# The product of wq and wo as 128 more columns of the gates' product

## The chip, the cores and the metric

The kernel runs on one core of a Trainium2 chip. The metric is the time of one execution on the device in microseconds (us); lower is better. Engines are named by their short names: PE is TensorE (matrix products), PEld its loading of weights, DVE is VectorE, ACT is ScalarE, POOL is GpSimd and SP is SyncE, which here only starts transfers.

## The reference, cut to what matters

Two layers, each a sum of an attention-like part and a feed-forward part over 8 x 256 tokens of 128 features. The first layer is a state-space block and a ternary feed-forward net. The second layer, in which the change lies, is:

```python
xn = _layernorm(x)
x  = x + attn(xn) + moe(xn)

# attn: per head (16 heads of 64), chunks of 64 tokens, W and b are a state that each chunk updates
xq, xk, xv = xn @ wq, xn @ wk, xn @ wv
Z1 = xk_c @ W + b;  lr = sigmoid(xk_c @ theta + theta_bias);  eta = token_eta * lr / 64
W, b = W - (eta * xk_c).T @ grad_x, b - sum(eta * grad_x)
Zq = xq_c @ W + b
out_c = xq_c + gamma * normalise(Zq) + beta
attn = concat(out) @ wo

# moe: 8 experts, the best 2 of each token by sigmoid(xn @ gate_w.T + gate_b), and a shared expert
```

Two consequences matter here. The term xq_c in out_c goes through wo unchanged, so its share of the result is xn @ (wq @ wo), a product with one matrix of 128 x 128. And the logits of the experts (8 columns) and of the rates lr (16 columns, from wk and theta) are also products of xn with a small matrix.

## The kernel before

The tokens are held as four chunks n (NCH) of four pairs of sequences bp (NBP): a tile is 128 rows, two sequences by 64 tokens. x1[n] is the residual stream of a chunk, 128 x 4 x 128 in SBUF; xnT[n] is its normalised and transposed form. All numbers are fp32.

The first layer runs first, with the order of all engines written out by hand (manual_schedule over all engines). Each chunk's feed-forward net is a list of steps (ffn_steps): first (two products and a silu), hidden (products and a gelu), mix and join, which end in residual, which adds the result to x1[n], and norm, which makes xnT[n] and lets POOL add the constant kc to x1[n]. Then come gates, scores and rates, the routing of the chunk's tokens: gates multiplies xnT[n] by gw, whose 24 columns are 8 for the experts and 16 for the rates; scores adds the bias and takes the sigmoid; rates makes eta and calls choose(0), the first choice of an expert; choose(1) makes the second choice and a product pn (all_ones and earlier times sel) that counts tokens; find_slots makes the slots from it. A function given to later() is put on a list that the next flush() runs, so gates, scores, rates and choose(1) come one flush apart, with steps of other work between them.

The chunks' steps are fillers in a main loop of turns. There are 16 units (chunk n, pair bp), and turn u works on three of them at once: z (unit u) makes states and gradients, g (unit u - 1) updates W and applies the queries, o (unit u - 2) writes out. For o the turn calls outputs_T (transposes the outputs, PE's poT and ACT's copy oT), then open_mix, mix_heads and residual:

```python
self.po = bank("po1")[:, :D]                       # open_mix: the opener, xn @ (wq wo)
nc.tensor.matmul(self.po, lhsT=xnT[self.n][:, self.bp, :], rhs=wqo, start=True, stop=False)
...                                                # mix_heads: eight products, oT by wo, into po
nc.vector.tensor_tensor(x, x, self.po, ALU.add)    # residual: x1[n][:, bp] += po
```

In the main loop the order of DVE and SP is the program's; that of PE, ACT and POOL is found by a scheduler that works with estimated times. The last turns are by hand again, for PE and ACT too. In turns 4, 5 and 14 to 16 the shared expert's pieces (shared_steps: a first part, pm and hid, and a second part, py) come in as fillers, in turn 5 also the routing of all tokens, and from turn 6 on the routed experts.

PSUM has two pools: bank() hands out one of four banks of 2 KB, two_banks() one of two pairs. A bank that is wanted waits until the last reader of an earlier tile in it is done. SBUF tiles named resident stay for the whole kernel: wqo, the product of wq and wo, is made once after the first layer and copied by ACT from PSUM.

Of the kernel before, what the change touches and what calls it, by code (L numbers as in the profile page):

```python
# [14 lines left out]
ALU = mybir.AluOpType  # L15
AX = mybir.AxisListType

P = 128
B, S, D = 8, 256, 128
# [4 lines left out]
H, HD, K = 16, 64, 64  # L24
HH = H // 2
NCH = S // K
NBP = B // 2
HC = H * HD
E = 8
# [31 lines left out]

C_EW2, C_EB1, C_EB2 = FF, 2 * FF, 2 * FF + 4
NEW = C_EB2 + D
I32 = mybir.dt.int32


# [12 lines left out]
def tile_two_layers(ctx: ExitStack, tc: tile.TileContext, t: dict, out: bass.AP):  # L79
    nc = tc.nc  # L80
# [10 lines left out]
    def bank(name):  # L91
        return ps1.tile([P, 512], F32, tag="bank", name=name)
# [4 lines left out]
    def resident(name, shape):  # L97
        return const.tile(shape, F32, tag=name, name=name)

    def resident_i(name, shape):  # L100
        return const.tile(shape, I32, tag=name, name=name)

    def load(name, shape, pool=const):
        sb = pool.tile(shape, F32, tag=name, name=name)
        nc.sync.dma_start(out=sb, in_=t[name])
        return sb
# [44 lines left out]
    x1 = [resident(f"x1_{n}", [P, NBP, D]) for n in range(NCH)]  # L151
    xnT = [resident(f"xnT_{n}", [P, NBP, P]) for n in range(NCH)]
# [27 lines left out]
    def later(f):  # L180
        pending.append(f)

    def flush():
        now, pending[:] = pending[:], []
        for f in now:
            f()
# [42 lines left out]
    gb = resident("gb", [P, E + H])  # L229

    def empty_rows(pool):
# [9 lines left out]
    nc.gpsimd.iota(  # L241
        second.bitcast(I32), [[P, NT]], base=B * S, channel_multiplier=1
    )
    nc.gpsimd.tensor_copy(second, second.bitcast(I32))
    wgt = resident("wgt", [P, NT, 2])
    eta = resident("eta", [P, NCH, NBP, H])
    te = resident("te", [P, 1])
    kc = resident("kc", [P, D])
    gw = resident("gw", [P, E + H])

    ready = []
    placed = []
# [13 lines left out]
    def ffn_steps(n):  # L266

        s = {}
# [58 lines left out]
        def norm():  # L327
            s["row"] = const.tile([P, NBP, ROW], F32, tag="xn1", name="xn1")
            s["xn"] = s["row"][:, :, 0:D]
            ln_apply_T(x1[n], s["stats"], s["xn"], xnT[n])  # L330
            nc.gpsimd.tensor_copy(s["row"][:, :, D], second[:, mine])
            nc.gpsimd.tensor_tensor(x1[n], x1[n], kc[:, None, :].to_broadcast([P, NBP, D]), ALU.add)
            later(gates)

        def gates():
            s["pg"] = bank("pg")[:, : NBP * (E + H)].rearrange("p (b c) -> p b c", b=NBP)
            for bp in range(NBP):
                nc.tensor.matmul(s["pg"][:, bp, :], lhsT=xnT[n][:, bp, :], rhs=gw, start=True, stop=True)
            later(scores)

        def scores():
            sg = small.tile([P, NBP, E + H], F32, tag="sg", name="sg")
            nc.vector.tensor_tensor(
                sg, s["pg"], gb[:, None, :].to_broadcast([P, NBP, E + H]), ALU.add
            )
            nc.scalar.activation(sg, sg, AF.Sigmoid)
            later(lambda: rates(sg))

        def rates(sg):
            nc.vector.tensor_scalar(eta[:, n], sg[:, :, E : E + H], te, None, ALU.mult)  # L350
            s["s"] = sg[:, :, 0:E]
            work = const.tile([P, 7, NBP * E], F32, tag="rt", name="rt")
            s["w"] = [work[:, i, :] for i in range(7)]
            choose(0)
            later(lambda: choose(1))

        def t_e(ap):
            return ap.rearrange("p (t e) -> p t e", e=E)
# [6 lines left out]
        def choose(k):  # L365

            shape = [P, NBP, E]
            left = t_e(s["w"][2]) if k else s["s"]
            m = wgt[:, mine, k]
            nc.vector.tensor_reduce(m, left, AX.X, ALU.max)  # L370
            eq = t_e(s["w"][k])
            nc.vector.tensor_tensor(eq, left, m.unsqueeze(2).to_broadcast(shape), ALU.is_equal)
            nc.vector.tensor_tensor(eq, eq, rank[:, None, :].to_broadcast(shape), ALU.mult)
            mr = small.tile([P, NBP], F32, tag="tk_mr", name="tk_mr") if k else s["row"][:, :, D + 1]
            nc.vector.tensor_reduce(mr, eq, AX.X, ALU.max)
            nc.vector.tensor_tensor(eq, eq, mr.unsqueeze(2).to_broadcast(shape), ALU.is_equal)
            if k == 0:
                nc.vector.scalar_tensor_tensor(t_e(s["w"][2]), eq, -4.0, s["s"], ALU.mult, ALU.add)
            else:
                sel = s["w"][3]  # L380
                nc.vector.tensor_tensor(sel, s["w"][0], s["w"][1], ALU.add)
                s["pn"] = bank("pn")[:, : 2 * NBP * E].rearrange("p (a c) -> p a c", a=2)
                nc.tensor.matmul(s["pn"][:, 0, :], lhsT=all_ones, rhs=sel, start=True, stop=True)
                nc.tensor.matmul(s["pn"][:, 1, :], lhsT=earlier, rhs=sel, start=True, stop=True)
                later(find_slots)
# [36 lines left out]
    with (  # L422
# [29 lines left out]
        wo = load("wo", [P, HH, D])  # L452
        headT = load("headT", [P, 2, HH], l0)
        wqT = load("wqT", [P, HH, D], l0)
        wq = load("wq", [P, HC])
        shared_w = resident("shared_w", [P, NEW])
        nc.sync.dma_start(out=shared_w, in_=t["moe_w"][E * P : NE * P, :])
        empty = empty_rows(l0)
        hp = [l0b.tile([P, B, S + 3], F32, tag="hp", name="hp") for half in range(2)]
# [54 lines left out]
        def convolve(half):  # L514
# [11 lines left out]
            return ins  # L526

        steps = ffn_steps(0)
        stats = {}
        layernorm0(0)  # L530
# [41 lines left out]
        for two in range(NBP // 2):  # L572

            pxp = bank("pxp").rearrange("p (b s) -> p b s", b=2)
            for half in range(2):
                for i in range(2):
                    b = 2 * (2 * two + i)
                    nc.tensor.matmul(
                        pxp[i * 64 : i * 64 + 64], lhsT=xp_w[:, half, :], rhs=hs[half][:, b : b + 2, :],
                        start=(half == 0), stop=(half == 1),  # L580
# [70 lines left out]
        for step in steps[12:14]:  # L651
            step()
        ffn1 = ffn_steps(1)

        pf = bank("pf")
        for hp_ in range(HH):
            nc.tensor.matmul(
                pf[:, 0:D], lhsT=wqT[:, hp_, :], rhs=wo[:, hp_, :], start=(hp_ == 0), stop=(hp_ == HH - 1)
            )
        wqo = resident("wqo", [P, D])  # L660
        nc.scalar.copy(wqo, pf[:, 0:D])

        pf2 = bank("pf2")[:, 0:D]
        for hp_ in range(HH):
            nc.tensor.matmul(
                pf2, lhsT=bpad[:, hp_, :], rhs=wo[:, hp_, :], start=(hp_ == 0), stop=(hp_ == HH - 1)
            )
        steps[14]()
        nc.vector.scalar_tensor_tensor(kc, shared_w[:, C_EB2:NEW], 0.1, pf2, ALU.mult, ALU.add)
        flush()  # L670
# [24 lines left out]
    def routing_steps():  # L695
        r = {}

        def work(name):

            return side["moe"].tile([P, NEW], F32, tag="ew", name=name, bufs=4)  # L700

        def constants():
            r["empty"] = empty_rows(side["moe"])
            w = r["w"] = work("rt_w")
            ints = w[:, 0:NJ].bitcast(I32)
            nc.gpsimd.iota(ints, [[1, NJ]], base=0, channel_multiplier=0)
# [110 lines left out]
    def expert_weights(j):  # L817
        if j < NJ:
            w = side["moe"].tile([P, NEW], F32, tag="ew", name=f"ew_{j}", bufs=4)
            r = nc.sync.value_load(wrow[0:1, j : j + 1], min_val=0, max_val=E * P)  # L820
# [11 lines left out]
    def routed_tokens_T(g):  # L832
        if g < NG:
            pt = bank("pxg")[:, : GJ * P].rearrange("p (j q) -> p j q", j=GJ)
            src = xg.pop(g)
            for j in range(GJ):
                nc.tensor.transpose(pt[:, j, :], src[:, j, 0:D], ident)
            ats[g] = side["moe"].tile([P, GJ], I32, tag="ats", name="ats", bufs=3)

# [42 lines left out]
    def routed_sums():  # L882
        for j, py in unsummed:
            g, i = divmod(j, GJ)
            if i == 0:
                ysum[g] = side["moe"].tile([P, GJ, D], F32, tag="ys", name="ys", bufs=3)
            nc.vector.tensor_tensor(ysum[g][:, i, :], py, ew.pop(j)[:, C_EB2:NEW], ALU.add)
            ready.append(lambda g=g, i=i: scatter_results(g, i))
        unsummed.clear()

    def scatter_results(g, i):
        assert g in known
        scattered.append(g * GJ + i)
        ins = transfer(
            out=y_dram, out_offset=bass.IndirectOffsetOnAxis(ap=ats[g][:, i : i + 1], axis=0),
            in_=ysum[g][:, i, :], in_offset=None, bounds_check=2 * B * S - 1, oob_is_err=False,
        )

        tc.declare_no_dep(ins, group="results", reason="distinct rows")
        tc.add_to_no_dep_group("results", ins)  # L900
# [23 lines left out]
    def result_steps(n, k):  # L924
# [3 lines left out]
        def fetch():  # L928
# [3 lines left out]
            elif n < NCH - 1:  # L932
                y = side["moe"].tile([P, NEW], F32, tag="ew", name="yc", bufs=4)[:, 0 : NBP * D]
            else:
# [38 lines left out]
    def pairs_of(heads):  # L973
        return slice(heads.start // 2, heads.stop // 2)
# [89 lines left out]
    class Unit:  # L1064
# [191 lines left out]

        def open_mix(self):
            self.po = bank("po1")[:, :D]
            nc.tensor.matmul(
                self.po, lhsT=xnT[self.n][:, self.bp, :], rhs=wqo, start=True, stop=False  # L1260
            )

        def mix_heads(self, k=ALL):
            part = pairs_of(k)
            for hp in range(part.start, part.stop):
                nc.tensor.matmul(  # L1266
                    self.po, lhsT=self.oT[:, hp, :], rhs=wo[:, hp, :], start=False,
                    stop=(hp == HH - 1),
                )

        def residual(self):
# [5 lines left out]
    fill = {u: [] for u in range(units + 2)}  # L1277
    gets = dict(RESULTS)
    steps = ffn1[EARLY:] + ffn_steps(2) + ffn_steps(3)
    for turn_u, k in FFN:  # L1280
        fill[turn_u] += [steps.pop(0) for _ in range(k)]
# [311 lines left out]
```

## Time and profile before

| what | us |
|---|---|
| median of 3 runs | 574.95 |
| lowest and highest | 573.02 and 576.1 |
| the profiled execution | 576.93 |
| its span, first to last instruction | 575.2 |
| PE busy in it | 534.9 |
| DVE busy in it | 405.0 |
| POOL busy in it | 296.3 |
| ACT busy in it | 259.0 |

The profile is that of one execution. A line of its timeline gives the start in us from the beginning of the span, the duration, the engine, the line of the kernel, the operation, what it writes and reads (output<-inputs), the shape, how many such instructions were merged (x16), and in brackets how long the engine had been idle before it and what ended that. A product in fp32 appears as two passes, so x2 is one product. Matrix passes overlap, and their ends are modelled, so their cost is read from the distance of their starts. A line of a table of stretches gives the stretch and its length, then for each of PE, PEld, DVE, ACT and POOL the busy time and the number of instructions, then the clock that PE was granted as a share of full speed, the share of the DMA engines' time, and GB/s.

### The profile page before, as it was taken

How to read it: one execution, taken by the hardware profiler on the slowest of the kernel's cores; microseconds unless marked ns; L12 is line 12 of the kernel's file. 1: busy time of each engine (PE TensorE's matmuls, PEld its weight loads, DVE VectorE, ACT ScalarE, POOL GpSimd, SP SyncE). 2: the span in 40 equal slices, each digit the busy share in tenths (PEclk: the TensorE clock that was granted, in tenths of full speed). 3: DMA queues.
4: the chain of work that ended last, by engine and by line, in shares of the span. 5: the costliest groups of instructions: out<-in, count | busy, mean ns of one | idle time of the engine just before them, and what ended most of it. 6: DMA issues, size and time to landing. Idle time of an engine off the chain costs nothing. (4 is left out here: it accounts for less than half of the span.)

```text
span 575.2 us, 14196 instructions
## 1 busy us (share of the span) xinstructions
PE 534.9 (93%) x5891; PEld 370.0 (64%) x5891; DVE 405.0 (70%) x649; ACT 259.0 (45%) x472; POOL 296.3 (52%) x258
## 2 busy tenths in 40 slices
PE   6999999999999999999978999999999999989695
PEld 3444655465556446476766787877787777878584
DVE  5597543647911675566969788869788777768995
ACT  5556444316420722314415363553546354453685
POOL 6216205750760176252774567465866646484861
PEclk9999999999999999898979999999999999999989
DMA  7901100000000000000152544352443434300322
GB/s 281 388 38 41 47 1 15 24 1 2 15 23 1 1 14 21 6 1 1 43 180 71 160 124 150 118 178 89 155 146 118 149 112 134 97 16 3 100 51 74
DMA packets 25200, 45.89 MB, mean 80 GB/s; under 512 B 3875, under 2 KB 16297, under 8 KB 24624
## 3 DMA queue, kind: packets, MB, share of 16 engines
q1 hardware_dynamic: 22864, 40.75, 21.9%
q0 software_dynamic: 2272, 4.24, 2.2%
q8 instruction: 46, 0.75, 0.5%
q14 instruction: 18, 0.15, 0.1%
HBM read 38.30 MB, written 7.13 MB: 79 GB/s over the span
## 5 line engine op out<-in xcount | busy, mean ns | idle before, releaser
L293 PE MATMUL pm<-g,h 128*128 128x512 f32 x256 | 115.3, 602 | 0.0
L175 POOL TENSOR_TENSOR rstd<-rs_v,neg_half 128x16 f32<-128x16 f32 x31 | 93.1, 3004 | 2.6
L293 PEld LDWEIGHTS pm<-g,h 128*128 128x128 f32 x256 | 48.7, 192 | 60.9 <-issue 58.1
L1118 POOL TENSOR_TENSOR gx<-xh,gam 128x1024 f32<-128x1024 f32 (+1 forms) x17 | 37.8, 2226 | 71.0 <-DVE er L1117 53.0
L866 ACT ACTIVATE rhid<-phd,ew 128x128 f32<-128x128 f32 x156 | 44.6, 373 | 41.3 <-issue 21.2
L174 POOL TENSOR_SCALAR rs_v<-var 128x16 f32<-128x16 f32 x31 | 7.3, 235 | 96.6 <-DVE var L1054 95.3
L297 ACT ACTIVATE g<-pm,cols 128x512 f32<-128x512 f32 x32 | 22.0, 687 | 77.1 <-PE pm L293 77.1
L163 POOL DMA_INDIRECT y_dram<-ys,ats x39 | 43.4, 1113 | 8.9 <-issue 8.8
L1054 DVE TENSOR_REDUCE var<-sq 128x16 f32<-128x1024 f32 (+1 forms) x33 | 38.9, 1181 | 9.4 <-ACT sq L1048 9.4
L861 PE MATMUL phd<-xgT,ew 128*128 128x128 f32 x312 | 43.4, 279 | 1.6 <-DMA ew<-in_moe_w 1.3
L861 PEld LDWEIGHTS phd<-xgT,ew 128*128 128x128 f32 x312 | 39.3, 191 | 8.0 <-issue 6.0
L1048 ACT ACTIVATE sq<-o 128x1024 f32<-128x1024 f32 (+1 forms) x17 | 17.1, 1009 | 55.1 <-DVE o L1037 55.1
L876 PE MATMUL pyr<-ew,rhid 128*128 128x128 f32 x312 | 41.4, 276 | 0.0
L163 POOL DMA_INDIRECT xg_dram<-xn,slot x32 | 35.9, 1121 | 8.6 <-issue 7.7
L1119 POOL TENSOR_TENSOR gx<-gx,u 128x1024 f32<-128x1024 f32 (+1 forms) x17 | 38.7, 2275 | 1.3
L876 PEld LDWEIGHTS pyr<-ew,rhid 128*128 128x128 f32 x312 | 38.0, 192 | 0.7 <-issue 0.5
L1094 DVE TENSOR_TENSOR u<-rows_b,pv 128x1024 f32<-128x1024 f32 x16 | 19.5, 1218 | 22.7 <-PE pv L982 22.7
L1266 PE MATMUL po<-wo,oT 128*128 128x128 f32 x256 | 33.1, 285 | 0.7 <-ACT oT L999 0.7
L1266 PEld LDWEIGHTS po<-wo,oT 128*128 128x128 f32 x256 | 32.0, 202 | 1.1 <-ACT oT L999 0.9
L982 PE MATMUL pk<-wk,xnT 128*128 128x512 f32 x64 | 31.4, 610 | 0.6 <-DVE xh L1037 0.4
L982 PE MATMUL pv<-wv,xnT 128*128 128x512 f32 x64 | 31.4, 613 | 0.0
L1011 PE MATMUL pq<-xnT,wq 128*128 128x256 f32 x128 | 30.8, 383 | 0.7 <-DVE B L1213 0.7
(233 smaller groups left out, 1067.7 us busy)
## 6 DMA issues: line engine op xcount, KB each, us to landing
ew<-in_moe_w SPq DMA_DIRECT2D x39, 578.0 KB
xg<-xg_dram SPq DMA_DIRECT2D x39, 65.0 KB
h<-in_h SPq DMA_DIRECT2D x2, 1024.0 KB
yc<-y_dram SPq DMA_DIRECT2D x6, 256.0 KB
rows_g<-in_rows_g SPq DMA_DIRECT2D x1, 1024.0 KB
rows_b<-in_rows_b SPq DMA_DIRECT2D x1, 1024.0 KB
w<-in_w SPq DMA_DIRECT2D x3, 256.0 KB
x<-in_x SPq DMA_DIRECT2D x3, 256.0 KB
```

Source lines behind the costliest of these rows:

```text
L163: ins = nc.gpsimd.indirect_dma_start(**what).ins
L175: turn[:] = [nc.gpsimd.tensor_tensor(dst, v[:, :width], neg_half[:, :width], ALU.pow).ins]
L293: nc.tensor.matmul(pm, lhsT=w[:, k, m * P : (m + 1) * P], rhs=s[src][:, k, :], start=(k == 0), stop=(k == 3),)
L861: nc.tensor.matmul(ph[:, ms], lhsT=w[:, ms], rhs=xgT[j // GJ][:, j % GJ, :], start=True, stop=True)
L866: nc.scalar.activation(hid[:, m, :], ph[:, ms], AF.Gelu, bias=w[:, C_EB1 + m : C_EB1 + m + 1])
L876: nc.tensor.matmul(py, lhsT=hid[:, m, :], rhs=w[:, C_EW2 + m * D : C_EW2 + (m + 1) * D], start=(m == 0), stop=(m == 3),)
L982: nc.tensor.matmul(pp[:, j, :], lhsT=xT, rhs=w[:, j * 512 : (j + 1) * 512], start=True, stop=True)
L1011: nc.tensor.matmul(pq[:, i, :], lhsT=wq[:, (h0 + i) * P : (h0 + i + 1) * P], rhs=xnT[n][:, 2 * half : 2 * half + 2, :], start=True, stop=True,
L1054: nc.vector.tensor_reduce(v[:, heads], sq[:, heads], AX.X, ALU.add)
L1118: nc.gpsimd.tensor_tensor(g, xh, gam2[:, k], ALU.mult)
L1119: turn[:] = [nc.gpsimd.tensor_tensor(g, g, self.t[:, k], ALU.add).ins]
L1266: nc.tensor.matmul(self.po, lhsT=self.oT[:, hp, :], rhs=wo[:, hp, :], start=False, stop=(hp == HH - 1),)
```

## The change

gw grows from 24 to 152 columns (NGW): its last 128 are the product of wq and wo, so wqo as a tile of its own goes. For chunks 0 to 2 gates multiplies by all 152 columns. Four pairs of 152 columns do not fit one bank of 512, so they go to two banks, two pairs in each; the bias is added in two halves. The product's last 128 columns are added to x1[n] by DVE in add_queries, two adds of 128 x 256, issued after choose(0) and ahead of choose(1). For these chunks open_mix only takes the bank, and the first product of mix_heads starts the sum. Chunk 3 keeps the narrow gates in one bank and its opener, which reads the 128 columns from gw.

```diff
+NGW = E + H + D
-    gw = resident("gw", [P, E + H])
+    gw = resident("gw", [P, NGW])
...
         def gates():
-            s["pg"] = bank("pg")[:, : NBP * (E + H)].rearrange("p (b c) -> p b c", b=NBP)
-            for bp in range(NBP):
-                nc.tensor.matmul(s["pg"][:, bp, :], lhsT=xnT[n][:, bp, :], rhs=gw, start=True, stop=True)
+            width, per = (E + H, NBP) if n == NCH - 1 else (NGW, 2)
+            s["pg"] = []
+            for b0 in range(0, NBP, per):
+                pg = bank("pg")[:, : per * width].rearrange("p (b c) -> p b c", b=per)
+                for i in range(per):
+                    nc.tensor.matmul(
+                        pg[:, i, :], lhsT=xnT[n][:, b0 + i, :], rhs=gw[:, 0:width], start=True, stop=True
+                    )
+                s["pg"].append((slice(b0, b0 + per), pg))
             later(scores)
         def scores():
             sg = small.tile([P, NBP, E + H], F32, tag="sg", name="sg")
-            nc.vector.tensor_tensor(
-                sg, s["pg"], gb[:, None, :].to_broadcast([P, NBP, E + H]), ALU.add
-            )
+            for pairs, pg in s["pg"]:
+                nc.vector.tensor_tensor(
+                    sg[:, pairs], pg[:, :, 0 : E + H],
+                    gb[:, None, :].to_broadcast([P, pg.shape[1], E + H]), ALU.add,
+                )
             nc.scalar.activation(sg, sg, AF.Sigmoid)
             later(lambda: rates(sg))
+        def add_queries():
+            for pairs, pg in s["pg"]:
+                x = x1[n][:, pairs, :]
+                nc.vector.tensor_tensor(x, x, pg[:, :, E + H : NGW], ALU.add)
         def rates(sg):
...
             choose(0)
             later(lambda: choose(1))
+            if n < NCH - 1:
+                add_queries()
...
-        wqo = resident("wqo", [P, D])
-        nc.scalar.copy(wqo, pf[:, 0:D])
+        nc.scalar.copy(gw[:, E + H : NGW], pf[:, 0:D])
...
         def open_mix(self):
             self.po = bank("po1")[:, :D]
-            nc.tensor.matmul(
-                self.po, lhsT=xnT[self.n][:, self.bp, :], rhs=wqo, start=True, stop=False
-            )
+            if self.n == NCH - 1:
+                nc.tensor.matmul(
+                    self.po, lhsT=xnT[self.n][:, self.bp, :], rhs=gw[:, E + H : NGW], start=True,
+                    stop=False,
+                )
...
-                    self.po, lhsT=self.oT[:, hp, :], rhs=wo[:, hp, :], start=False,
-                    stop=(hp == HH - 1),
+                    self.po, lhsT=self.oT[:, hp, :], rhs=wo[:, hp, :],
+                    start=(hp == 0 and self.n < NCH - 1), stop=(hp == HH - 1),
```

## The prediction

> **What bounds the kernel now.** I read the page first, then the waits of TensorE (PE), then the timeline around the lines that the change touches, then the order of instructions of the changed kernel as built, which shows what stands where on each engine and holds no times.
>
> ```profile
> PE 534.9 (93%) x5891; PEld 370.0 (64%) x5891; DVE 405.0 (70%) x649; ACT 259.0 (45%) x472; POOL 296.3 (52%) x258
> ...
> PEclk9999999999999999898979999999999999999989
> ```
>
> The span is 575.2 us, and PE is the bound: 93% busy; the clock line shows full speed nearly throughout. Its idle gaps over 0.08 us sum to some 30 us, and from 72 to 530 us hardly one is over 1.3 us, with one exception below. So PE time taken out there should come off the end, and DVE time (70%) should cost only where PE waits for it.
>
> What the change takes out and what it widens:
>
> ```profile
> 168.39 0.38 PE L1259 MATMUL po<-wqo,xnT 128*128 128x128 f32 x2
> 168.61 1.95 PE L1266 MATMUL po<-wo,oT 128*128 128x128 f32 x16
> ...
> 71.39 0.97 PE L338 MATMUL pg<-gw,xnT 128*128 128x24 f32 x8
> 71.39 0.86 PEld L338 LDWEIGHTS pg<-gw,xnT 128*128 128x128 f32 x7 [0.24 <-issue]
> ```
>
> A product in fp32 is two passes. The opener at 168.39 holds PE until the next product starts at 168.61: 0.22 us for two passes of 128 columns, 0.11 each. The durations in the second column include the drain of a pass and must not be summed. A pass of only 24 columns is no cheaper: seven weight loads in 0.86 us, six pitches in 0.67, again 0.11 us. So the weight load sets the pace of both.
>
> The exception, in turn 5 of the main loop (the turn in which the tokens are routed):
>
> ```profile
> 284.97 1.22 DVE L1247 TENSOR_TENSOR o<-o,rstd 128x1024 f32<-128x1024 f32 x1
> ...
> 286.33 0.72 PE L995 MATMUL poT<-ident,o 64*128 64x64 f32 x16
> ...
> 290.65 0.84 ACT L790 ACTIVATE hid<-pm,shared_w 128x256 f32<-128x256 f32 x2 [6.75 <-remote]
> 291.38 1.01 ACT L999 COPY oT<-poT 128x1024 f32<-128x1024 f32 x1
> 291.54 2.08 PE L784 MATMUL pm<-xnT,shared_w 128*128 128x256 f32 x4 [4.49 <-ACT hid L790]
> ```
>
> ScalarE (ACT) stands still for 6.75 us although its input has been ready since about 286.2; PE then stands for 4.49 us. The table of stretches shows the second price, the granted clock (the column before the last two):
>
> ```profile
> 289.00:292.40 3.40, 0.86 (x2) 0.77 (x3) 3.30 (x4) 1.74 (x3) 3.24 (x3) 0.50 0.29 83
> 292.40:295.80 3.40, 3.40 (x15) 3.13 (x15) 2.15 (x4) 0.84 (x2) 2.04 (x1) 0.50 0.76 243
> 295.80:299.00 3.20, 3.20 (x74) 3.08 (x76) 0.29 (x1) 0.00 (x0) 3.07 (x2) 1.00 0.94 336
> ```
>
> From 291.5 to 295.8 PE works at half speed: about 2.1 us lost.
>
> **The change part by part.** (1) Openers removed: 12 of 16 (chunks 0 to 2), 12 x 0.22 = -2.64 us. They lie in turns 2 to 13, where PE is the bound. (2) Gates widened: 12 products, 24 passes, from 24 to 152 columns. Passes of 512 columns follow each other at 0.43 us (16 of L293 in 7.03 us), so 152 columns are 0.127 us by proportion; with a little for issue I take 0.131, +0.02 each: +0.48 us. Ends: +0.016 (pure proportion) and +0.035. Here a rule speaks against the change. The Trainium skill, "TensorE: Matmul & The Clock Gate", section "Back-to-back issue gap", gives the isolated gap as columns over the clock plus a small constant, so work grows with columns. Scaled from our 0.43 us, 24 columns would have cost 0.02 us, and the widening 24 x 0.107 = 2.57 us: the whole saving gone. The row says 0.11 for the narrow pass, because every pass here loads new weights; I take the row. By the rule my sum would be 2.1 us later.
>
> (3) On DVE, per chunk: the add of the bias in two halves of 128x48 instead of one of 128x96 (0.258 us; a 128x32 takes 0.19), +0.15; and two adds of 128x256 from PSUM. The row L806 has this shape, two streams and a PSUM source: 0.416 us each. Together +0.98 us, three times 2.9 us, all before 200 us. They stand between choose(0) and choose(1). They also wait for GpSimd's add of kc to the same x1: it ended at 70.8, 131.3 and 192.0, five us before it is needed, so that wait is free. SyncE's and GpSimd's orders are unchanged; no DMA is added.
>
> (4) Buffers: the gates now take two of four PSUM banks and hold them until DVE has added the queries, not until the bias is added. Chunk 0: the next hidden product takes a bank that ACT must free (its silu ends at 74.04, later by the wider gates) and began at 74.00: I allow +0.25. Chunk 1: the scheduler has moved 29 of 32 products of z ahead of the pair that needs the bank. The adds end near 136.7 and 137.2, PE arrives at 136.9, and DVE's sel, 139.84 before, comes at about 140.4 for a PE that asks at 140.7: 0. Chunk 2 has no such cover:
>
> ```profile
> 197.86 0.74 DVE L283 SCALAR_TENSOR_TENSOR g<-p,cols,gs 128x512 f32<-128x512 f32 x1
> ...
> 199.63 0.19 DVE L381 TENSOR_TENSOR rt<-rt 128x32 f32<-128x32 f32 x1
> ...
> 199.88 0.41 PE L383 MATMUL pn<-rt,all_ones 128*128 128x32 f32 x2 [0.37 <-DVE rt L381]
> ```
>
> PE already waits here for DVE's sel, so everything added ahead of it on DVE shows: 0.85 for the adds and 0.16 for the shifted gates. sel moves from 199.82 to about 201.0. Behind pn wait the hidden products of chunk 3. Beyond the width, counted in (2), +1.0 us (0.4 to 1.8).
>
> (5) Turn 5 is reordered by the scheduler, because the opener no longer opens the bank early. In before the last shared pieces stood between the first shared product and poT: opener, second part, first part. Now poT and the output product follow directly, and one first part and one second part of the shared expert go behind z. PE is through at 282.9 and poT needs o, ready at 286.2: a hole of 3.4 us. poT is then done at 287, and the output product needs ACT's oT. If ACT stands until 290.6 as before, oT is there at 291.7, PE idles another 4.7 us, and the half clock runs to 295.8 again. Then output product, second part, first part (4.5 us of work, 2.05 us for the clock), so pw starts at 298.2 as before, but with 0.9 + 1.8 us of shared work still to do. That work fills the 1.6 us of gaps that before has between 302 and 307.5. Net +1.5 us (0 to +5).
>
> Is ACT's stand really going to come again? In the window 289 to 291 of the DMA view there is one packet on an instruction queue, and ACT goes on shortly after:
>
> ```profile
> q14 instruction: 1, 0.01, 2.4%
> ```
>
> So it looks like a late load of code, behind the writes of empty rows and scattered rows of those microseconds. The Trainium skill, "Runtime: NRT & Kernel Launch", section "Instruction fetch mechanics", calls the crossing of a code block mostly hidden. By that rule the stand would be an accident and gone in the new run. The trace shows 6.75 us; ACT's instruction count is the same and so is the traffic, so I let it return.
>
> (6) Elsewhere two expert products instead of one stand between output product and pw in three turns: 0.22 us, just the place that the opener had. Nothing.
>
> Sum: -2.64 + 0.48 + 0.25 + 1.0 + 1.5 = +0.6 us on a profiled execution of 576.93 us (span 575.2 and 1.7 around it). On the median of 574.95 us: 575.5.
>
> **The rivals.** A (likeliest): the saving on PE is spent in chunk 2 and turn 5: 575.5, by its own bounds 573.2 to 577.5.
> B: ACT's code arrives in time. Then oT comes at 288.1, PE has idled 4.5 us instead of 8, loses some 1.7 us in one slow stretch of 3.4 us, and pw starts at 294.3: 3.9 us earlier than in A, 571.6; without the slow stretch 569.9. For it: the packet's delay is a matter of what shares its queue, and this reordering shifts that. Against: same code, same traffic.
> C, slower: the clock decides. With PE idle from 282.9 rather than 287, half speed begins one stretch earlier and, if poT's short burst restarts nothing, the recovery falls one later; each stretch of 3.4 us costs 1.7 us, and the pending shared work then no longer fits into later gaps (+1.6): 575.5 + 1.7 + 1.6 = 578.8, with a second stretch 580.5. It decides once PE's hole ahead of poT exceeds some 2 us. The same can strike in chunk 2, where some 1 us of new holes lies close together. For it: the half clocks of 289 and 545 us follow holes of PE of 4.5 and 3.3 us. Against: a hole of 1.25 us at 306 brought none, and the one of turn 5 has its two slow stretches already.
> D: the two banks stall PE longer than I read, by a silu that comes late in each of three chunks, 1 us each: 578.5.
> E, the change does not do what it says: the wide pass costs in proportion to its columns: 577.6.
>
> **How the numbers follow.** A 0.47, B 0.20, C 0.24, D and E 0.09 together. About 0.5% (2.9 us) is what a measurement of this kernel can tell from no change: below 572.1 or above 577.8. B gives most of faster (0.13), with a little from A's low side if chunk 2 and turn 5 are cheap: 0.17. C gives most of slower (0.22), D and E 0.06, A's far side 0.05: 0.33. The rest is 0.50. The range takes in B's first value and C with its second stretch: 570.5 to 581.0.
>
> **What would show it.** Gates passes at a pitch of 0.13 us (0.21 would be E); no opener in chunks 0 to 2; pn of chunk 2 near 201 us after a wait for sel of about 0.9 us; pm in chunk 0 starting by 74.5; in turn 5 a wait of PE for o of about 3 us and then one for oT, with ACT still; half clock to about 296. I am wrong if turn 5 has no hole (then the median is below 573), or if new half clocks stand near 200 us.

## The result and the profile after

| what | before | after |
|---|---|---|
| median, us | 575.32 (12 runs) | 578.84 (12 runs) |
| lowest to highest, us | 573.02 to 577.11 | 577.37 to 581.61 |
| ratio after/before, 95% interval | | 1.0068 (1.0052 to 1.0085) |
| the profiled execution, us | 576.93 | 577.46 |

The change costs 0.68% by the ratio, and the medians lie 3.5 us apart. Three later sets of runs, each on one chip, measured it again: 1.0022 (1.0003 to 1.0041); +2.2 us between the medians of two kernels that carry the same addition on ACT; and 1.0050 (1.0033 to 1.0067) to before, or +2.5 us between two kernels with the same addition. So the sign is settled, and the size is some 1 to 4 us.

The pair of profiled executions differs by 0.5 us only: that of before lies 1.6 us above its median, that of after 1.4 below. The two profiles show where things moved. They don't show the size.

The page of after, its busy times and the line of the granted clock:

```profile
PE 534.4 (93%) x5867; PEld 368.9 (64%) x5867; DVE 407.7 (71%) x658; ACT 259.1 (45%) x472; POOL 297.8 (52%) x258
...
PEclk9999999999999999998979999999999999999989
```

PE has 24 passes less and DVE 9 instructions more, as the diff says. PE's busy time is hardly shorter (534.4 after 534.9).

The timeline of PE around the gates of chunk 0 and of chunk 2, with DVE's two adds of chunk 2:

```profile
72.25 1.20 PE L344 MATMUL pg<-gw,xnT 128*128 128x152 f32 x8
73.29 1.02 PE L280 MATMUL p<-xnT,w 128*128 128x512 f32 x2
74.15 1.02 PE L281 MATMUL p<-xnT,w 128*128 128x512 f32 x2
75.09 1.12 PE L295 MATMUL pm<-g,h 128*128 128x512 f32 x2
...
193.24 1.28 PE L344 MATMUL pg<-gw,xnT 128*128 128x152 f32 x8
...
197.49 1.12 PE L280 MATMUL p<-xnT,w 128*128 128x512 f32 x2 [0.40 <-ACT gs L283]
...
199.52 0.74 DVE L363 TENSOR_TENSOR x<-x,pg 128x256 f32<-128x256 f32 x2
...
202.20 0.41 PE L401 MATMUL pn<-rt,all_ones 128*128 128x32 f32 x2 [0.17 <-DVE rt L399]
202.44 0.39 PE L402 MATMUL pn<-rt,earlier 128*128 128x32 f32 x2
202.67 3.68 PE L295 MATMUL pm<-g,h 128*128 128x512 f32 x8
```

In chunk 0 eight passes of 152 columns take 1.04 us from the first to what follows, 0.130 each. In chunk 2 PE waits 0.40 us for a silu of ACT (gs), which has to free a bank; the gates hold two of the four until the adds are done, 199.52 to 200.26. PE's wait for DVE's sel, 0.37 us before, is 0.17. The same place in before:

```profile
191.72 1.05 PE L338 MATMUL pg<-gw,xnT 128*128 128x24 f32 x8
...
200.35 5.83 PE L293 MATMUL pm<-g,h 128*128 128x512 f32 x13
```

Turn 5 in the same timeline, with ACT's copy that the output product needs:

```profile
281.37 1.89 PE L801 MATMUL pm<-xnT,shared_w 128*128 128x256 f32 x8
286.58 1.12 PE L1012 MATMUL poT<-ident,o 64*128 64x64 f32 x16 [3.32 <-DVE o L1264]
290.36 3.78 PE L1285 MATMUL po<-wo,oT 128*128 128x128 f32 x16 [2.66 <-issue]
293.93 3.10 PE L816 MATMUL py<-shared_w,hid 128*128 128x128 f32 x16
296.87 1.03 PE L801 MATMUL pm<-xnT,shared_w 128*128 128x256 f32 x4
297.83 1.16 PE L1210 MATMUL pw<-gx,xk 64*64 64x64 f32 x64
...
289.29 1.01 ACT L1016 COPY oT<-poT 128x1024 f32<-128x1024 f32 x1 [5.10 <-remote]
```

There are now two holes, 3.32 us ahead of the transposes and 2.66 ahead of the output product, where before had one of 4.49. The view names no wait for the second (issue), but ACT's copy ends at 290.30, just ahead of it. The half clock lasts a stretch longer:

```profile
286.10:289.50 3.40, 1.12 (x16) 0.96 (x16) 3.19 (x9) 0.21 (x1) 2.79 (x3) 0.50 0.28 83
289.50:292.90 3.40, 2.54 (x12) 2.54 (x13) 3.33 (x3) 0.81 (x1) 3.24 (x3) 0.50 0.27 78
292.90:296.30 3.40, 3.40 (x18) 3.40 (x18) 2.09 (x5) 0.00 (x0) 2.00 (x2) 0.50 0.88 279
296.30:299.50 3.20, 3.20 (x76) 2.51 (x76) 0.45 (x1) 0.84 (x2) 3.12 (x2) 1.00 0.88 317
```

### The profile page after: what moved, and what is told of

It is laid out like the page before. It is cut to its first block, busy times and chain, and to the rows that moved or that the text cites. A ratio compares the mean times of both kernels' runs of the same rounds, so it can differ in the third digit from the quotient of the medians.

```text
span 575.7 us, 14166 instructions
## 1 busy us (share of the span) xinstructions
PE 534.4 (93%) x5867; PEld 368.9 (64%) x5867; DVE 407.7 (71%) x658; ACT 259.1 (45%) x472; POOL 297.8 (52%) x258
## 5 line engine op out<-in xcount | busy, mean ns | idle before, releaser
L295 PE MATMUL pm<-g,h 128*128 128x512 f32 x256 | 113.7, 595 | 0.0
L164 POOL DMA_INDIRECT y_dram<-ys,ats x39 | 44.8, 1149 | 8.9 <-issue 8.5
```

What stands on the lines that cost most here:

```text
L164: ins = nc.gpsimd.indirect_dma_start(**what).ins
L295: nc.tensor.matmul(pm, lhsT=w[:, k, m * P : (m + 1) * P], rhs=s[src][:, k, :], start=(k == 0), stop=(k == 3),)
```

## The experiments

Ratios are to the kernel before on the same chip, with the 95% interval. The first four kernels shared one chip (before: 573.6 us), the next four another (575.36), the last four a third (555.77).

**Taking the change apart.** The changed kernel once more:

> The changed kernel once more, for a second profile and its granted clock. Measured so far: 578.84 us, ratio 1.0068; but its profiled execution was 577.46 us, at the low end. Theory T (turn 5 and the gates of chunk 2 spend what the openers save): ratio 1.005 to 1.008, the profile again shows PE idle ahead of poT in turn 5 for about 3.3 us, and again ahead of the output product for 2.5 to 5 us, depending on how long ACT stands. Rival K (the clock): where the run is slower than 577.5, it holds one or two more stretches of half clock than the six of the profile before; otherwise the PE gaps sum to 2 to 4 us more than the 30.7 us of the first profile.

Measured: 574.44 us, 1.0022 (1.0003 to 1.0041). Then the openers alone; what they would have contributed is left out of the sum:

```diff
             self.po = bank("po1")[:, :D]
-            nc.tensor.matmul(
-                self.po, lhsT=xnT[self.n][:, self.bp, :], rhs=wqo, start=True, stop=False
-            )
+            if self.n == NCH - 1:
+                nc.tensor.matmul(
+                    self.po, lhsT=xnT[self.n][:, self.bp, :], rhs=wqo, start=True, stop=False
+                )
```

> The kernel before with the 12 openers of chunks 0 to 2 taken out and nothing put in their place (their product is left out of the result). The scheduler gives turn 5 the new order of the changed kernel. Theory T: -2.6 us for the openers and +1.5 to +3.5 us for turn 5, so 573.5 to 576.5 us, ratio 0.997 to 1.002. Rival G (the gates and adds cost all, turn 5 nothing): -2.6 us, ratio 0.9955. Rival K: a further stretch or two of half clock after turn 5's hole, ratio 1.002 to 1.006.

Measured: 572.56 us, 0.9989 (0.9966 to 1.0012). Twelve openers of 0.22 us are gone, and the time falls by some 0.6 us, if at all. The other part alone, the changed kernel with all openers kept (the product is then added twice):

```diff
-            if self.n == NCH - 1:
+            if True:
                 nc.tensor.matmul(
...
-                    start=(hp == 0 and self.n < NCH - 1), stop=(hp == HH - 1),
+                    start=False, stop=(hp == HH - 1),
```

> The changed kernel with all openers kept (so the product of wq and wo is added twice in chunks 0 to 2): the wide gates, the two banks and the six adds on DVE alone, turn 5 in the order of before. Theory T: +0.5 us for the width and +1.3 to +2 us for the waits in chunks 0 and 2, so about +2 us, ratio 1.003 to 1.004. Rival G: +6 us, ratio 1.010, since the openers then give their 2.6 us in full. Rival E (passes in proportion to columns): at least +2.6 us for the width alone, ratio 1.006 or more.

Measured: 574.86 us, 1.0033 (1.0012 to 1.0055): the wide gates and the adds cost +1.9 us. The parts sum to +1.3 us, which is what the whole change measured on this chip (0.22% of 573.6). Last, the changed kernel with one opener kept, that of the unit written out in turn 5, and its pair left out of the wide add. This puts PE's order in turn 5 back to that of before:

```diff
+                k = 1 if n == 0 and pairs.stop == NBP else 2
+                x = x1[n][:, pairs.start : pairs.start + k, :]
+                nc.vector.tensor_tensor(x, x, pg[:, 0:k, E + H : NGW], ALU.add)
...
+        def opens(self):
+            return self.n == NCH - 1 or self.u == ROUTE - 2
...
```

> The changed kernel with one opener kept: that of unit 3, in turn 5; its pair is left out of the wide add, so the result is whole. The built order of turn 5 is then that of before. Theory T: the cost of turn 5 goes, 0.2 us comes back: 574.5 to 577 us, ratio 0.998 to 1.003, and no PE gap of 3 us ahead of poT. Rival G: as the changed kernel, ratio 1.007.

Measured: 571.84 us, 0.9988 (0.9963 to 1.0012), 0.34% or 2.0 us below the changed kernel on the same chip (2.6 us by the medians). One product of 0.22 us put back takes 2 us off. The waits of PE in turn 5, first without the openers, then with the one kept:

```profile
282.47 0.71 PE L995 MATMUL poT<-ident,o 64*128 64x64 f32 x16 [3.31 <-DVE o L1247]
285.29 3.78 PE L1267 MATMUL po<-wo,oT 128*128 128x128 f32 x16 [2.11 <-ACT oT L999]
```

```profile
283.96 0.71 PE L1013 MATMUL poT<-ident,o 64*128 64x64 f32 x16
288.20 2.08 PE L802 MATMUL pm<-xnT,shared_w 128*128 128x256 f32 x4 [3.54 <-ACT hid L808]
```

The two holes come with the removal of the openers and not with the wide gates. When the one opener is back, one hole of 3.54 us stands in their place, as in before. The clock differs too. In the second trace of the changed kernel half speed lasts three stretches here, with the one opener kept it lasts one:

```profile
282.90:286.30 3.40, 1.12 (x16) 0.96 (x16) 3.23 (x8) 0.00 (x0) 2.65 (x3) 0.50 0.27 81
286.30:289.70 3.40, 2.20 (x10) 2.20 (x11) 3.30 (x4) 1.01 (x1) 3.24 (x3) 0.50 0.33 98
289.70:293.10 3.40, 3.40 (x18) 3.40 (x18) 2.16 (x3) 0.00 (x0) 2.36 (x1) 0.50 0.87 249
```

```profile
287.90:291.30 3.40, 3.10 (x10) 2.74 (x11) 2.90 (x4) 2.04 (x4) 3.32 (x2) 0.50 0.42 83
291.30:294.70 3.40, 3.40 (x51) 3.28 (x53) 1.51 (x3) 0.00 (x0) 2.00 (x2) 1.00 0.95 358
```

The reordered turn 5 is shown as the cause of 2 us.

**Is ACT's stand in turn 5 a late load of code?** The prediction said so. 24 tiny copies were added to ACT's program in chunk 0, so that another instruction stands at the place where the stand comes; the order on PE and DVE is unchanged.

```diff
             nc.scalar.activation(s[dst][:, m, :], pm, AF.Gelu, scale=cols[:, c + m : c + m + 1])
+            if n == 0:
+                for _ in range(3):
+                    nc.scalar.copy(root, norm_eps)
```

> The kernel before with 24 tiny copies of one element on ACT in chunk 0's hidden steps, where ACT waits for PE; PE's and DVE's orders stay as they were. They move every later instruction of ACT 24 places on in its code. Theory L (ACT's stand in turn 5 is a late load of code, behind the row writes of that moment): the stand leaves turn 5, PE's hole of 3.5 to 4.5 us there and most of its half clock go, -3 to -6 us, ratio 0.990 to 0.995, unless the new place hits other traffic. Rival S (ACT waits for a semaphore or a buffer): no change, ratio 0.999 to 1.001, hole and half clock as before.

Measured: 577.22 us, 1.0029 (1.0010 to 1.0048). The stand is where it was, and so is PE's hole:

```profile
290.20 0.84 ACT L793 ACTIVATE hid<-pm,shared_w 128x256 f32<-128x256 f32 x2 [6.51 <-remote]
```

```profile
291.09 2.08 PE L787 MATMUL pm<-xnT,shared_w 128*128 128x256 f32 x4 [4.46 <-ACT hid L793]
```

The same copies in the changed kernel, and in the one with turn 5's opener kept:

> The changed kernel with the same 24 copies. Theory L: the second hole of turn 5 (2.4 to 2.7 us ahead of the output product) shrinks to about 1.1 us, that of 3.3 us ahead of poT stays, since it waits for DVE's o; one or two stretches of half clock go: ratio 0.993 to 0.999 to the kernel before. Rival S: as without the copies, 1.002.

Measured: 579.38 us, 1.0072 (1.0041 to 1.0102).

> The changed kernel with the opener of turn 5 kept, and the 24 copies: a candidate that may beat both. Theory L: what before_pad gives and what the kept order gave (ratio 0.9988) add up: 0.988 to 0.994. Rival S: 0.9988.

Measured: 576.18 us, 1.0022 (1.0006 to 1.0038). Before pays 0.29% for the copies, and in both kernels with before's order in turn 5 PE's hole is 4.46 us. The packet on the instruction queue q14 speaks against the theory as well. With the copies, four packets of q14 come 25 to 31 us earlier than in before, one of them at 282.8 instead of 312.2 us:

```profile
q14 instruction: 1, 0.01, 3.0%
```

That is the DMA view of before with the copies, 282 to 284 us, where before has no such packet. The packet beside the stand does not move with them (289.2 in before, 288.7 with the copies), so by these traces it does not belong to ACT's code. A load of ACT's code does not hold ACT. What ACT waits for is PE's signal, as the semaphore events of the trace say: in before, the last pass of the shared product is over by its modelled end at 286.20, and PE's update for it is recorded at 290.56; in the kernel with the copies at 290.11.

Beside these, before without 11 openers, turn 5's kept (the product left out again for those 11):

```diff
-            nc.tensor.matmul(
...
+            if self.n == NCH - 1 or self.u == ROUTE - 2:
+                nc.tensor.matmul(
```

> The kernel before with 11 of 12 openers taken out (their product is left out of the result), that of turn 5 kept, so that turn 5 keeps its order. Theory T: the openers' price in full, 11 x 0.22 = -2.4 us, ratio 0.9958. Rival H (openers partly stand in time that PE would have waited anyway): -1 us, ratio 0.998; then turn 5 cost less than 2 us in no_openers.

Measured: 574.19 us, 0.9986 (0.9963 to 1.0009), so -0.8 us (-2.1 to +0.5) where 11 x 0.22 = -2.4 was expected. The interval misses the full saving by a little; the paragraph on the openers, further down, comes back to it.

**What holds PE's signal?** During the stand, SyncE writes eight blocks of empty rows and GpSimd scatters eight blocks. The first kernel writes all empty rows early in the first layer, by copies from DRAM to DRAM, and drops the eight writes. The order on PE, DVE, ACT and GpSimd stays.

```diff
+        for row in range(0, E * CAP, behind):
+            rows = min(behind, E * CAP - row)
+            nc.sync.dma_start(
+                out=xg_dram[row : row + rows, :], in_=xg_dram[E * CAP : E * CAP + rows, :]
+            )
...
-                ins = nc.sync.dma_start(out=xg_dram[bass.ds(reg, P), :], in_=r["empty"]).ins
```

> Before, with the rows for tokens that no expert has copied from DRAM to DRAM early in the first layer (20 copies) in place of SyncE's eight writes in turn 5, whose row is read from a register; everything else, and the order on PE, DVE, ACT and GpSimd, as in before. In before PE's own completion signal in turn 5 comes 3.4 to 4.4 us after the modelled end of its last pass, while SyncE's eight writes (281.57 to 291.14) and GpSimd's eight scatters (to 289.96) run. Theory R (SyncE's writes hold it): ACT's stand of 6.5 us falls to about 2, PE's hole of 4.46 us to under 1, and one or two stretches of half clock go: 0.989 to 0.994. Theory S (the scatters hold it): stand and hole as before, 0.998 to 1.002. Theory N (neither): the same as S.

Measured: 556.09 us, 1.0006 (0.9994 to 1.0019). ACT's stand is not in its trace. The second kernel keeps the eight writes and lets the scatters go in three groups:

```diff
         if u == ROUTE:
-            transfers(len(ready))
+            transfers(1)
...
+        if u == ROUTE:
+            transfers(len(ready))
         filler()
```

> Before with SyncE's eight writes in place, but GpSimd's eight scatters of turn 5 let go in three groups (3, 3 and 2) between other steps of the turn in place of one run; the order on PE, DVE, ACT and SyncE as in before. R: stand and hole at most 0.5 us shorter, 0.998 to 1.002. S: the stand breaks up, PE's hole falls below 2 us, 0.990 to 0.997, unless GpSimd's own work comes later. N: 0.998 to 1.003 with the hole as before.

Measured: 562.27 us, 1.0118 (1.0093 to 1.0143). The stand is absent here too, with SyncE's writes in place. But neither absence says anything of its cause, because before itself takes 555.77 us on this chip, 20 us less than on the others, and gains nothing from the early rows. Its mean granted clock over 38 runs is 0.9947, and with the early rows 0.9949; the two slow stretches that follow the stand in the first profile would take some 0.006 off. So before very probably has no stand here either, though no trace of it on this chip exists. Neither theory was tested: the thing to be explained didn't occur. The second kernel is slower for a plain reason, in its waits of PE; the late scatters make the rows come late:

```profile
300.23 0.33 PE L837 MATMUL pxg<-ident,xg 128*128 128x128 f32 x1 [4.05 <-DMA xg<-xg_dram]
```

What the third chip gives is better than what was asked of it: the change without the stand. The changed kernel with early rows, and the one that also keeps turn 5's opener:

> The changed kernel with the same early copies. R: the hole ahead of the output product in turn 5 (2.4 to 2.7 us) falls to about 1, the hole of 3.3 us ahead of the transposes stays, because it waits for DVE: 0.995 to 1.001 of before. S and N: holes as in the changed kernel, 1.002 to 1.007. In both the distance to before_early_rows is at least that of the changed kernel to before.

> The changed kernel with unit 3's opener kept (turn 5 in before's order), and the same early copies. R: 0.987 to 0.993, the fastest of all. S and N: 0.997 to 1.001, as without the copies.

Measured: 558.63 us, 1.0050 (1.0033 to 1.0067), and 555.08 us, 0.9987 (0.9977 to 0.9997). Against before with the same rows (556.09) the change costs 558.63 - 556.09 = +2.5 us; with turn 5 in its old order it gains 1.0. Turn 5 alone is worth 3.55 us. Its timeline in before with early rows:

```profile
279.89 1.03 PE L783 MATMUL pm<-xnT,shared_w 128*128 128x256 f32 x4
281.05 0.71 PE L994 MATMUL poT<-ident,o 64*128 64x64 f32 x16
281.91 1.13 PE L783 MATMUL pm<-xnT,shared_w 128*128 128x256 f32 x4
282.88 2.04 PE L1265 MATMUL po<-wo,oT 128*128 128x128 f32 x16
284.75 1.95 PE L798 MATMUL py<-shared_w,hid 128*128 128x128 f32 x16
287.67 1.16 PE L1192 MATMUL pw<-gx,xk 64*64 64x64 f32 x64 [0.97 <-DVE gx L1133]
```

And in the changed kernel with early rows:

```profile
276.73 1.89 PE L800 MATMUL pm<-xnT,shared_w 128*128 128x256 f32 x8
281.94 0.71 PE L1011 MATMUL poT<-ident,o 64*128 64x64 f32 x16 [3.31 <-DVE o L1263]
283.75 3.57 PE L1284 MATMUL po<-wo,oT 128*128 128x128 f32 x16 [1.10 <-ACT oT L1015]
```

Without the stand the old order has no hole ahead of poT or of the output product: opener and shared products lie under DVE's and ACT's work. The first hole is one of 0.97 us ahead of pw. The new order leaves PE idle for 3.31 and 1.10 us. The price continues in the clock. Old order first, then new, the stretch in which the output product runs:

```profile
282.80:286.20 3.40, 3.40 (x31) 3.34 (x30) 3.33 (x3) 0.85 (x3) 2.94 (x4) 1.00 0.95 377
```

```profile
283.60:287.00 3.40, 3.25 (x15) 3.25 (x16) 3.33 (x3) 0.10 (x1) 2.94 (x4) 0.50 0.96 384
```

At half the clock PE gets through 15 passes where it got through 31. Over all runs on that chip the mean granted clock is 0.9949 for before with early rows, 0.9901 for the changed kernel and 0.9944 with turn 5's opener. A half-speed stretch of 3.41 us takes 3.41 x 0.5 / 556 = 0.0031 off the mean, so the changed kernel has 0.0043 / 0.0031 = 1.4 stretches more per run than with the opener kept. At 1.7 us each that is 2.4 of the 3.55 us. The pair of traces agrees: from the shared product that both have ahead of the turn's holes (at 277.25 with the opener kept, 276.73 without) to the transposes pxkT (299.36 and 301.13) it is 22.11 and 24.40 us. Of these 2.3 us, 1.5 are the output product at half the clock (3.57 us; with the opener kept 2.04); the other 0.8 I put down to what is left of 4.4 us of holes once the postponed shared work has filled later gaps. The kernel with turn 5's opener is the only one that is faster than before beyond its interval, by 0.7 us.

**Turn 5's order on the three chips.** On each chip there is a pair of changed kernels, with turn 5's opener kept and without it, that differ in this order (and in the half of one add on DVE). On the second chip both carry the 24 copies, on the third both have the early rows.

| chip | order of before, us | new order, us | difference, us | mean granted clock, old and new order | half clock in turn 5 in the two traces, us |
|---|---|---|---|---|---|
| first | 571.84 | 574.44 | 2.6 | 0.9884, 0.9853 | 3.41, 10.24 |
| second | 576.18 | 579.38 | 3.2 | 0.9877, 0.9818 | 3.41, 10.24 |
| third | 555.08 | 558.63 | 3.55 | 0.9944, 0.9901 | 0, 3.41 |

By the ratios the differences are 2.0, 2.9 and 3.5 us. On the first two chips the old order has the stand, on the third it has not, and the step costs 2 to 3.5 us all the same. By the mean clocks the new order has 1.0, 2.0 and 1.4 stretches of half speed more per run. At 1.7 us each, an estimate, they would be most of the difference on every chip.

## Why the prediction was right, and where its steps were off

The measured median, 578.84 us, lies in the range given, but above the bounds of the likeliest case A (573.2 to 577.5). The sign of A (a small loss) and the places held. The size did not: +0.6 us in the sum, some 1 to 4 measured. The term that was too small is turn 5, and rival C names what it left out.

**Openers, -2.64.** It holds where it can be read without turn 5. In the first turn with an opener, 10.62 us lie between the hidden products and the output product in before (157.99 to 168.61), and 10.40 in after (159.73 to 170.13): 0.22 less. On the first chip, the changed kernel with all openers kept and that with turn 5's alone differ in eleven openers (and in the half of one add on DVE). The medians lie 3.0 us apart, by the ratios it is 2.6; eleven at 0.22 are 2.4. On the third chip, with turn 5 undisturbed, the gain is 1.0 us, where these 2.4 and the gates' 1.7 (below) leave 0.7. Only on the second chip did eleven openers taken out of before give less, 0.8, with a wide interval. Whether part of the saving is lost there stays open.

**Gates, +0.48 for the width.** The new passes are at 0.130 us in chunk 0, where 0.131 was predicted. The term is still small by some 0.2 us: the narrow passes came at 0.101 (71.39 to 72.20, eight passes), not 0.11, so a chunk pays 0.23 or 0.22 and not 0.16. The prediction used only the formula of the section "Back-to-back issue gap" ("TensorE: Matmul & The Clock Gate" in the Trainium skill) and so had a rule against its row. The same section says that in a stream of weight loads and products both set the spacing, and that the formula for an isolated product comes out too low for few columns. That agrees with the row here, where every pass loads new weights. Rival E falls with the pitch.

**Waits around the gates, +0.25 and +1.0.** From the gates' first pass to a product behind the routing (pn in chunk 0, pm in chunks 1 and 2) PE took 9.48, 9.63 and 8.63 us in before, and 9.81, 10.18 and 9.43 in after: 0.33, 0.55 and 0.80 more, together 1.7 us. Of this 0.67 is width. Beyond it the three chunks lose 0.10, 0.33 and 0.58, where 0.25, 0 and 1.0 were predicted. Part of chunk 1's loss is that PE now switches between products of z and p once more. In chunk 2 the place was wrong: it is the silu that must free a bank, 0.40 us, and not sel, whose wait shrank. The sum of the two terms, 1.73, fits the 1.7, partly by luck, since errors of both signs cancel. Measured alone the part is +1.9 (0.7 to 3.2). Rival D, with 1 us for each chunk, is not borne out.

**Turn 5, +1.5.** In the pair of profiles many figures came true: a hole of 3.4 us (3.32), o ready at 286.2 (poT at 286.58), half clock to 295.8 (296.3), pw at 298.2 (297.83). The second hole, behind ACT, is 2.66 and not 4.7: PE's signal for the transposes came only 1.6 us after their modelled end. The step that was mis-sized is the clock. The working let half speed end where it ended in before, so it charged turn 5 no slow stretch beyond the two of before. Rival C did, by way of a hole that opens earlier, and the traces show it: half speed begins at 286.1 instead of 289.0 us and lasts three stretches. On each of the three chips the new order has one or two stretches more, and the whole step costs 2.0 to 3.55 us. The bound of 0 to 5 holds this; the 1.5 taken in it was too low. The stand of 4.49 us in the profile that the term was worked out from does not explain the miss, since on the second chip the old order stands too (4.46 us) and the step costs some 3 us.

C's threshold, a hole of some 2 us, was not measured. That its 578.8 is also the median of the first set of runs is in part luck: by the parts, turn 5 (2.0 to 3.55), gates (1.7) and openers (-2.6) sum to +1.1 to +2.6 us, and how the 3.5 us of that set divide was not measured, since its two profiles are only 0.5 us apart.

**ACT's stand as a load of code.** Wrong, by two runs. Neither the stand nor the packet beside it moved when ACT's code was moved. And an instruction packet crosses in turn 5 of before with early rows as well, where ACT doesn't stand at all (DMA view, 283 to 285 us):

```profile
q14 instruction: 1, 0.01, 1.0%
```

So the section "Instruction fetch mechanics" of "Runtime: NRT & Kernel Launch" in the Trainium skill, which calls such crossings mostly hidden, agrees with the runs, and weighing it against the stand was no argument either way. Rival B was built on the same reading and let only the changed kernel lose the stand. On the third chip the traces with early rows are both without it, and the change still costs 2.5 us.

## What to carry to other kernels

A small product that looks like pure cost may be what an order hangs on: here an opener of 0.22 us let a scheduler place 3 us of other work under a wait, and taking it out of that one turn cost ten times its length or more. Before an instruction on the busiest engine is removed, ask what is placed by it, and compare the new order with the old in the stage with the longest wait. And where the new order opens a hole on that engine, price the hole together with the stretches of half clock that follow it in the traces: here they were most of the cost, and the hole alone looked cheap, because postponed work filled later gaps.

## What the runs showed of the hardware that was not expected

Before took 573.6 to 575.4 us in three sets of runs and 555.8 in the fourth, on another chip. Part of the difference can be seen. In before, PE's products of 64 x 64 are broken by waits for nothing that the profile shows, and a stretch of half clock follows (the granted clock is 0.56 from 231.4 to 234.8 us):

```profile
228.91 0.36 PE L1026 MATMUL pzq<-W,xqT 64*64 64x64 f32 x5 [0.39 <-issue]
229.68 0.33 PE L1026 MATMUL pzq<-W,xqT 64*64 64x64 f32 x4 [0.41 <-issue]
230.43 0.35 PE L1026 MATMUL pzq<-W,xqT 64*64 64x64 f32 x3 [0.42 <-issue]
230.71 5.40 PE L293 MATMUL pm<-g,h 128*128 128x512 f32 x8
```

On the quick chip the same products run through, and the eight passes behind them take 3.70 us and not 5.40:

```profile
227.67 1.16 PE L1025 MATMUL pzq<-W,xqT 64*64 64x64 f32 x64
228.76 3.70 PE L293 MATMUL pm<-g,h 128*128 128x512 f32 x8
```

PE's breaks of this kind sum to 5.8 us in the trace of before and, on the quick chip, to nothing but one of 0.48 us in one kernel; the stand of PE's signal in turn 5 is missing there too. They may have one cause; no run shows it, and what holds the signal stays open.

Half speed came in stretches of 3.41 us or a multiple of it in every trace, but for a last one that the end cuts off. How long it lasts follows PE's busy time in these stretches. Of the 53 whole ones in the 14 traces, each that had PE busy for 0.87 of its time or more was followed by full speed (37), and each with 0.77 or less by another at half (16). So two holes in a row can cost more than one: in turn 5 of after the three slow stretches have PE busy for 1.12, 2.54 and 3.40 us of 3.40, and only the third ends the half clock.
